# adaLN, Mamba2 and binarized FFN in one kernel: layer norms applied by ScalarE, gates' rows on other engines and another queue, weight tiles a step later

## The chip, the cores and the metric

The kernel runs on one core of a Trainium2 chip. A core has TensorE (PE; its weight load is shown apart as PEld), VectorE (DVE), ScalarE (ACT), GpSimd (POOL) and SyncE (SP). Each takes its instructions in order from its own queue; they meet through semaphores. Transfers are issued by SyncE, and a few by GpSimd and ScalarE, and are carried out by 16 DMA engines. The metric is device time in microseconds (us); lower is better. The time before is 733.64 us, the median of three runs between 733.6 and 734.45.

## The reference

There are 4 batches of 512 tokens with 512 features, all float32. With a modulation vector of six parts per batch (sa, ca, ga, sb, cb, gb), the block computes:

```
mod = (silu(c) @ wmod) -> sa, ca, ga, sb, cb, gb
ga = (2*(ga >= 0) - 1) * maximum(abs(ga), 0.25)      # gb likewise
h = layernorm(x) * (1 + ca) + sa
x = x + ga * mamba(h)
h = layernorm(x) * (1 + cb) + sb
x = x + gb * ffn(h)
layernorm(x) = (x - mean) / sqrt(var + 1e-5)
mamba(h): xBCzA = h @ in_proj.T;  xBC = silu(conv4(xBC) + bias)
          y = chunk scan with chunks of 128, decays exp(segsum(-softplus(A)))
          out = (y + D * x / dt) * silu(z + z_bias) @ out_proj.T
ffn(h):   bw = where(w >= 0, 1, -1) * mean(abs(w), per row);  h @ bw.T + bias
```

There are 64 heads of 16, 8 groups with a state of 64, an inner width of 1024, and a convolution over 2048 channels.

## The kernel before, in words

The 2048 tokens are worked in 8 halves (`h`) of 256 tokens; two halves make a batch. A half has two chunks of 128 (`c` = 0 and 1), and the scan of a chunk is cut into four units (`gp`), so there are 64 units, one per step of the main loop. Python lists (`FIRST`, `SECOND`, `FRONT`, and the calls of `at` behind them) say which other piece of work is laid into which step; the program is then put in order at build time, engine by engine, and runs in that order.

The front of half h+1 runs beside the scan of half h: load of x (`load_x`, L79), layer norm (`f_norm`, L307; it calls `layer_norm`, L289), four transposes on TensorE (`phT`, L330), modulation on ScalarE (`hT`, L347), dt (`f_dt`: `pa`, L368, then a chain of small VectorE work), projections B, C, x0 to x3 in pairs (`pp_B`, `pp_C`, `pp_x`, L434), each followed by ScalarE's first tap (`u_B`, `u_C`, `u_x`, L450), three VectorE taps per tile (L454), tanh (L458) and a product (L459). The z projections are evacuated by ScalarE (`uz`, L516; `thz`, L520). `xs` (L507) is a product on GpSimd with rows `rr` that SyncE loads (L502).

A unit (`stage0`, `stage1`, `stage2`) loads two decay tiles (SyncE, L541 and L542), takes 16 exponentials of 128x128 (ScalarE, L549, eight per tile), multiplies by the masked C-B products (VectorE, L625, once per tile), and multiplies with x on TensorE (`py`, L212 and L215). `yt` and `z` follow on VectorE and GpSimd (L666 to L675). Four decay tiles exist, so two units are in flight. The state rows `e` are loaded by SyncE (L582).

The tail of a chunk: `tail1` (L729) makes the out projection `po` (L739), `t = po * gates` (L742), the residual sum (L743), the layer norm of one tile, and adds the gated FFN bias on GpSimd (L745); `tail2` transposes (`ph`, L757) and modulates (`h`, L759); `tail3` makes `pf` (L775) and the output. The tails of chunk c=0 and of c=1 lie in the units that follow them.

`layer_norm` runs its statistics on VectorE (L295, L296), adds the epsilon (L297), takes the power -0.5 on GpSimd (`rs_a`, `rs_f`, L298), and applies both mean and scale on VectorE (L300). There are 32 applies of 128x512: 16 on x, two per half, and 16 on t, one per chunk.

Near the start, beside half 0, `late_mods` (L233) makes the other four modulation parts (`pg`, `rows`, `pm`) and then the gates' rows: five VectorE operations on 64x512 (L256 to L260) and three stores to `gate_d` in DRAM on the SyncE queue (L262). `load_gates` (L719) reads them back, broadcast, into `gates`. `load_wout` (L265) loads the out projection. `signs` (L269) loads a block of FFN weight rows `fw` (L272), sums their absolute values (`alpha`, L274), takes the sign (L277) and scales it on ScalarE (`sw`, L278); `turned_signs` (L281) transposes it into `bwT`.

What one bank of PSUM each holds (`mm` tiles: projections, transposes, po, pf) goes round five buffers, handed out in program order: a TensorE product waits until the readers of the tile five back are done. The steps around the change are set by these lines:

```
at(1, behind, 0, late_mods)
at(2, load_wout)
for o in range(NK):
    at(o // 2 + 2, signs, o)
...
for o in range(NK):
    at(o // 2 + 5, behind, 1, turned_signs, o)
```

Of the kernel before, what the change touches and what calls it, by code (L numbers as in the profile page):

```python
# [11 lines left out]
F32 = mybir.dt.float32  # L12
AF = mybir.ActivationFunctionType
# [3 lines left out]
P = 128  # L17
# [23 lines left out]
def adaln_mamba_block(  # L41
# [139 lines left out]
    def load_late(h):  # L181

        load_wm_at(2, wout[:, 0:NK])
        load_wm_at(5, wout[:, NK:])
        load_wm_at(4, bwT)
        for k in range(2):
            load_wm_at(3, room_z[k].unsqueeze(1), k)
        load_wm_at(3, room[:, 0:2, :], 2)


    sc = keep.tile([P, NK, 32], F32, name="sc")
# [41 lines left out]
    def late_mods(h):  # L233

        pg = ps.tile([P, DM], F32, tag="mm", name="pg")
        glued([
            partial(
                mm, pg[32 * j : 32 * j + 32, :], sc[:, k, :], wms[t6, k], start=(k == 0), stop=(k == NK - 1)
            )
            for k in range(NK) for j, t6 in enumerate((2, 5, 4, 3))  # L240
        ])
        row = wk.tile([P, DM], F32, tag="t", name="rows", bufs=1)
        nc.vector.tensor_copy(row, pg)
        pm = ps.tile([P, NK, P], F32, tag="mm", name="pm")
        for dt in range(NK):
            nc.tensor.transpose(pm[:, dt, :], row[:, dt * P : (dt + 1) * P], ident)
        nc.vector.tensor_copy(modT[:, 2], pm[:, :, 96 : 96 + B])
        nc.vector.tensor_scalar(modT[:, 3], pm[:, :, 64 : 64 + B], 1.0, None, ALU.add)

        g = row[0:64, :]  # L250
        sg = wk.tile([64, DM], F32, tag="h2", name="sg")
        ab = wk.tile([64, DM], F32, tag="h2", name="ab")
        brow = wk.tile([64, DM], F32, tag="th", name="brow")
        second = slice(32, 32 + B)
        nc.sync.dma_start(brow[second, :], ffn_b.partition_broadcast(B))
        nc.vector.tensor_scalar(sg, g, 0.0, 2.0, ALU.is_ge, ALU.mult)  # L256
        nc.vector.scalar_tensor_tensor(ab, g, -1.0, g, ALU.mult, ALU.max)
        nc.vector.tensor_scalar(ab, ab, 0.25, None, ALU.max)
        nc.vector.scalar_tensor_tensor(sg, sg, -1.0, ab, ALU.add, ALU.mult)
        nc.vector.tensor_mul(ab[second, :], sg[second, :], brow[second, :])  # L260
        for i, v in enumerate((sg[0:B, :], sg[second, :], ab[second, :])):
            nc.sync.dma_start(gate_d[:, i, :], v)  # L262

    def load_wout():
        nc.sync.dma_start(wout, w_outT.rearrange("(k p) e -> p k e", p=P))  # L265
# [23 lines left out]
    def layer_norm(tiles, name, into=None):  # L289
        n = len(tiles)  # L290
        st = wk.tile([P, n, 6], F32, tag=f"st{n}", name=f"st_{name}")
        mv = wk.tile([P, n, 2], F32, tag=f"mv{n}", name=f"mv_{name}")
        rs = wk.tile([P, n], F32, tag=f"rs{n}", name=f"rs_{name}")
        for j, t in enumerate(tiles):
            nc.vector.bn_stats(st[:, j, :], t)  # L295
            nc.vector.bn_aggr(mv[:, j, :], st[:, j, :])  # L296
        nc.vector.tensor_scalar(rs, mv[:, :, 1], EPS, None, ALU.add)  # L297
        nc.gpsimd.tensor_tensor(rs, rs, mhalf[:, :n], ALU.pow)  # L298
        for j, t in enumerate(tiles):
            nc.vector.tensor_scalar(  # L300
                into[j], t, mv[:, j, 0:1], rs[:, j : j + 1], ALU.subtract, ALU.mult
            )


# [512 lines left out]
    for h in range(NHALF):  # L817
# [4 lines left out]
        if h == 0:  # L822
            at(0, load_late, h)
            at(1, behind, 0, late_mods)
            at(2, load_wout)
            for o in range(NK):
                at(o // 2 + 2, signs, o)
    for o in range(NK):
        at(o // 2 + 5, behind, 1, turned_signs, o)
    for h in range(NHALF):  # L830
# [75 lines left out]
```

## Time and profile before

| what | value |
|---|---|
| median of three runs | 733.64 us |
| the profiled execution, its own time | 737.38 us |
| span of the profile | 735.7 us |
| mean granted TensorE clock | 0.993 |
| busy TensorE, VectorE, ScalarE, GpSimd | 700.4, 599.5, 522.0, 254.8 us |
| layer norm applies on VectorE (L300) | 11.5 us in 16 (t), 9.8 us in 16 (x) |
| VectorE idle before the t applies, waiting for GpSimd's power | 12.8 us in 16 |
| exponentials of the decays on ScalarE (L549) | 293.9 us in 960 |

The profile is one execution; every row has a start or a sum in microseconds. A busy share is an average over stages. An idle time is put down to what ended last before it ended, "waiter <- releaser". Matmuls are pipelined, so a busy TensorE is not one at its peak; the granted clock is given beside it by stage. The profiled execution is 0.5% longer than the median; 1.7 us of it lie outside the span.

### The profile page before, as it was taken

Reading aid. Unit: us, or ns where it says so; the run is one execution under the profiler, and the core shown is the slowest. Engines: PE = TensorE matmul, PEld = TensorE weight load, DVE = VectorE, ACT = ScalarE, POOL = GpSimd, SP = SyncE. Lnnn points to the kernel's source line nnn. Section 1 sums busy time; section 2 is a strip of 40 time slices with the busy share of each in tenths; the row PEclk is TensorE's granted clock in tenths of the full one; section 3 lists DMA queues with packets and bytes.
Section 4 is the critical chain, followed back from the end, with each engine's and each line's share of the span. In section 5 each row is a group of like instructions: output and inputs, shape, how many; then the busy total and the mean of one; then the engine's idle time right before and its main releaser. Section 6 shows DMA issues by size and latency. Waiting matters only on the chain.

```text
span 735.7 us, 15007 instructions
## 1 busy us (share of the span) xinstructions
PE 700.4 (95%) x5196; PEld 500.8 (68%) x5196; DVE 599.5 (81%) x1170; ACT 522.0 (71%) x1507; POOL 254.8 (35%) x297
## 2 busy tenths in 40 slices
PE   6999979899999999999999999999999999999997
PEld 3786746666677666677677666776667866677754
DVE  3869888876998678986899768996799867996995
ACT  2467658748696697785976787865968768788941
POOL 4021323444243332343223342433414332333652
PEclk9999989999999999999999999999999999999999
DMA  8991693535555256444644256552564537457720
GB/s 279 328 291 41 204 208 85 135 98 142 127 132 144 63 155 137 102 115 102 159 116 130 53 116 168 142 137 53 140 132 114 130 86 176 116 150 151 142 69 29
DMA packets 119067, 99.24 MB, mean 135 GB/s; under 512 B 73984, under 2 KB 97152, under 8 KB 118992
## 3 DMA queue, kind: packets, MB, share of 16 engines
q1 hardware_dynamic: 117808, 96.39, 52.3%
q0 software_dynamic: 896, 1.38, 0.7%
q8 instruction: 41, 0.67, 0.4%
q10 hardware_dynamic: 288, 0.52, 0.2%
q14 instruction: 34, 0.28, 0.1%
HBM read 92.47 MB, written 5.79 MB: 134 GB/s over the span
## 4 chain that ended last, share of the span: by engine, by line
PE 65%; ACT 16%; DVE 9%; DMA 4%; issue 4%; POOL 1%; SPq 1%; ACTq 0%; DVEq 0%; POOLq 0%
PE po L739 14%; PE pp_x L434 11%; PE pp_z L434 10%; ACT decay L549 9%; PE pp_C L434 7%; PE pp_B L434 5%; PE pf L775 3%; PE py L212 2%; PE py L215 2%; DVE decay L625 2%; ACT h L759 2%; DVE u_x L454 2%; DMA fw<-in_ffn_w 2%; ACT win L549 2%; PE gy L215 2%
## 5 line engine op out<-in xcount | busy, mean ns | idle before, releaser
L549 ACT ACTIVATE decay<-decay,st 128x128 f32<-128x128 f32 x960 | 293.9, 395 | 4.2 <-DMA decay<-sums_d 3.7
L625 DVE SCALAR_TENSOR_TENSOR decay<-decay,gm 128x1024 f32<-128x1024 f32 x120 | 160.8, 1341 | 50.3 <-ACT decay L549 47.2
L434 PE MATMUL pp_x<-hT,win 128*128 128x259 f32 x512 | 120.7, 390 | 7.3 <-DVE u_C L454 7.3
L434 PE MATMUL pp_z<-hT,win 128*128 128x256 f32 x512 | 118.1, 383 | 0.0
L434 PEld LDWEIGHTS pp_x<-hT,win 128*128 128x128 f32 x512 | 96.9, 193 | 25.2 <-ACT decay L549 7.7
L739 PE MATMUL po<-wout,z 128*128 128x512 f32 x256 | 113.8, 595 | 0.0
L434 PEld LDWEIGHTS pp_z<-hT,win 128*128 128x128 f32 x512 | 94.3, 189 | 16.3 <-issue 3.5
L675 POOL TENSOR_TENSOR z<-yt,z 128x256 f32<-128x256 f32 x62 | 62.9, 1015 | 76.1 <-DVE yt L674 57.8
L454 DVE SCALAR_TENSOR_TENSOR u_x<-pp_x,cw,u_x 128x256 f32<-128x256 f32 x192 | 83.6, 474 | 1.3 <-ACT u_x L450 0.7
L739 PEld LDWEIGHTS po<-wout,z 128*128 128x128 f32 x256 | 47.5, 190 | 53.1 <-issue 52.4
L672 POOL TENSOR_TENSOR yt<-yt,xs 128x256 f32<-128x256 f32 x46 | 41.4, 899 | 106.3 <-DVE yt L671 78.6
L507 POOL TENSOR_TENSOR xs<-u_x,rr 128x512 f32<-128x512 f32 x32 | 42.7, 1334 | 79.2 <-DVE u_x L459 61.3
L516 ACT ACTIVATE uz<-pp_z,zb 128x256 f32<-128x256 f32 x64 | 27.5, 470 | 59.0 <-PE pp_z L434 59.0
L215 PE MATMUL py<-decay,xpad 128*32 128x128 f32 x1680 | 66.3, 276 | 0.0
L434 PE MATMUL pp_B<-hT,win 128*128 128x259 f32 x256 | 63.5, 396 | 2.7 <-ACT decay L549 1.9
L434 PE MATMUL pp_C<-hT,win 128*128 128x259 f32 x256 | 59.6, 384 | 1.1 <-DVE u_x L454 1.1
L775 PE MATMUL pf<-bwT,h 128*128 128x512 f32 (+1 forms) x136 | 59.0, 578 | 1.4 <-ACT h L759 1.3
L434 PEld LDWEIGHTS pp_B<-hT,win 128*128 128x128 f32 x256 | 47.4, 193 | 14.5 <-ACT decay L549 3.1
L450 ACT ACTIVATE u_x<-pp_x,cb,cw 128x256 f32<-128x256 f32 x64 | 35.3, 560 | 30.5 <-PE pp_x L434 30.4
L434 PEld LDWEIGHTS pp_C<-hT,win 128*128 128x128 f32 x256 | 47.8, 189 | 9.4 <-PE pn L424 1.4
L679 POOL TENSOR_TENSOR xd<-xpad,st 128x256 f32<-128x256 f32 x48 | 34.1, 727 | 55.8 <-PE pst L215 28.3
L212 PE MATMUL py<-decay,xpad 128*32 128x128 f32 x240 | 47.4, 279 | 3.2 <-issue 2.2
(157 smaller groups left out, 1080.9 us busy)
## 6 DMA issues: line engine op xcount, KB each, us to landing
decay<-sums_d SPq DMA_DIRECT2D x120, 256.0 KB
decay<-sums_d SPq DMA_DIRECT2D x120, 128.0 KB
rr<-r_d SPq DMA_DIRECT2D x64, 128.0 KB
e<-e_d SPq DMA_DIRECT2D x96, 64.0 KB
win<-in_w_inT SPq DMA_DIRECT2D x4, 1024.0 KB
xr<-in_x SPq DMA_DIRECT2D x16, 256.0 KB
res<-o SPq DMA_DIRECT2D x15, 256.0 KB
x<-in_x SPq DMA_DIRECT2D x14, 256.0 KB
```

The source lines that it names most:

```text
L212: first = products[0]()
L215: product()
L434: last = mm(pm, win[:, k, col : col + P], H[h]["hT"][:, k, lo:], start=(k == 0), stop=(k == NK - 1))
L450: nc.scalar.activation(u[:, j, :], pm[:, KS - 1 :], AF.Identity, bias=cb[:, t : t + 1], scale=cw[:, t, KS - 1 : KS])
L454: nc.vector.scalar_tensor_tensor(u[:, j, :], pm[:, k : k + T], cw[:, t, k : k + 1], u[:, j, :], ALU.mult, ALU.add)
L507: nc.gpsimd.tensor_tensor(xs, xc, rr, ALU.mult)
L549: nc.scalar.activation(ets[r][:, i, :], ets[r][:, i, :], AF.Exp, bias=H[h]["st"][:, hd : hd + 1], scale=-1.0)
L625: nc.vector.scalar_tensor_tensor(ets[r], ets[r], 1.0, bc_mid(gm[:, r, :], HPG), ALU.min, ALU.mult)
L672: ew.tensor_add(t, t, xs)
L675: ew.tensor_mul(zg, t, zg)
L739: last_po = mm(po, H[h]["z"][g // 2][:, g % 2, c * CH : (c + 1) * CH], wout[:, g, :], start=(g == 0), stop=(g == NKI - 1))
L775: mm(pf, h2[:, k, :], bwT[:, k, cols], start=(k == 0), stop=(k == NK - 1))
```

## The change

Three things change. First, every layer norm but the very first (`a0`) is applied by ScalarE as `rs * t + nm` with a per-partition bias `nm = -mean * rs`. VectorE makes `-mean`, GpSimd multiplies it by `rs` after the power, and ScalarE applies. Second, the gates' rows leave `late_mods` for a function of their own, `late_gates`, one step later: VectorE does the sign, ScalarE the absolute value, GpSimd the three others, and the stores go through GpSimd's queue; the work stands in the `gates` buffer (`room`) itself, and the load of the FFN bias row moves to `load_late`. Third, `signs` runs one step later; `turned_signs` stays.

In the program order built from it, ScalarE's t apply in a c=0 tail of halves 1 to 6 stands after the first exponential of the next unit's first decay tile. The x applies and the t of c=1 stand between `thz_1` and `uz_2`. In half 1's front the order on ScalarE is: the absolute value, eight exponentials, the two x applies, eight exponentials, `uz_3`, `xpad`, `thz_3`, eight exponentials, the first `hT`, eight exponentials, the other three `hT`. On TensorE, `pf` of a c=0 tail stands ahead of `gy` in five halves, and the PSUM buffers are handed out anew.

```diff
--- before.py
+++ after.py
@@ -186,6 +186,7 @@
         for k in range(2):
             load_wm_at(3, room_z[k].unsqueeze(1), k)
         load_wm_at(3, room[:, 0:2, :], 2)
+        nc.sync.dma_start(brow[second, :], ffn_b.partition_broadcast(B))
 
 
     sc = keep.tile([P, NK, 32], F32, name="sc")
@@ -246,20 +247,28 @@
             nc.tensor.transpose(pm[:, dt, :], row[:, dt * P : (dt + 1) * P], ident)
         nc.vector.tensor_copy(modT[:, 2], pm[:, :, 96 : 96 + B])
         nc.vector.tensor_scalar(modT[:, 3], pm[:, :, 64 : 64 + B], 1.0, None, ALU.add)
-
-        g = row[0:64, :]
-        sg = wk.tile([64, DM], F32, tag="h2", name="sg")
-        ab = wk.tile([64, DM], F32, tag="h2", name="ab")
-        brow = wk.tile([64, DM], F32, tag="th", name="brow")
-        second = slice(32, 32 + B)
-        nc.sync.dma_start(brow[second, :], ffn_b.partition_broadcast(B))
-        nc.vector.tensor_scalar(sg, g, 0.0, 2.0, ALU.is_ge, ALU.mult)
-        nc.vector.scalar_tensor_tensor(ab, g, -1.0, g, ALU.mult, ALU.max)
-        nc.vector.tensor_scalar(ab, ab, 0.25, None, ALU.max)
-        nc.vector.scalar_tensor_tensor(sg, sg, -1.0, ab, ALU.add, ALU.mult)
-        nc.vector.tensor_mul(ab[second, :], sg[second, :], brow[second, :])
+        late_row.append(row)
+    late_row = []
+    second = slice(32, 32 + B)
+    brow = room[0:64, 2, :]
+    def late_gates(h):
+        g = late_row.pop()[0:64, :]
+        sg, ab = room[0:64, 0, :], room[0:64, 1, :]
+        nc.vector.tensor_scalar(sg, g, 0.0, 0.5, ALU.is_ge, ALU.subtract)
+        nc.scalar.activation(ab, g, AF.Abs)
+        nc.gpsimd.tensor_scalar(ab, ab, 0.25, 2.0, ALU.max, ALU.mult)
+        nc.gpsimd.tensor_tensor(sg, sg, ab, ALU.mult)
+        nc.gpsimd.tensor_tensor(ab[second, :], sg[second, :], brow[second, :], ALU.mult)
         for i, v in enumerate((sg[0:B, :], sg[second, :], ab[second, :])):
-            nc.sync.dma_start(gate_d[:, i, :], v)
+            nc.gpsimd.dma_start(gate_d[:, i, :], v)
 
     def load_wout():
         nc.sync.dma_start(wout, w_outT.rearrange("(k p) e -> p k e", p=P))
@@ -295,10 +304,21 @@
             nc.vector.bn_stats(st[:, j, :], t)
             nc.vector.bn_aggr(mv[:, j, :], st[:, j, :])
         nc.vector.tensor_scalar(rs, mv[:, :, 1], EPS, None, ALU.add)
+        if name == "a0":
+            nc.gpsimd.tensor_tensor(rs, rs, mhalf[:, :n], ALU.pow)
+            for j, t in enumerate(tiles):
+                nc.vector.tensor_scalar(
+                    into[j], t, mv[:, j, 0:1], rs[:, j : j + 1], ALU.subtract, ALU.mult
+                )
+            return
+        nm = wk.tile([P, n], F32, tag=f"nm{n}", name=f"nm_{name}")
+        nc.vector.tensor_scalar(nm, mv[:, :, 0], -1.0, None, ALU.mult)
         nc.gpsimd.tensor_tensor(rs, rs, mhalf[:, :n], ALU.pow)
+        nc.gpsimd.tensor_mul(nm, nm, rs)
         for j, t in enumerate(tiles):
-            nc.vector.tensor_scalar(
-                into[j], t, mv[:, j, 0:1], rs[:, j : j + 1], ALU.subtract, ALU.mult
+            nc.scalar.activation(
+                into[j], t, AF.Identity, bias=nm[:, j : j + 1], scale=rs[:, j : j + 1]
             )
 
 
@@ -823,8 +843,9 @@
             at(0, load_late, h)
             at(1, behind, 0, late_mods)
             at(2, load_wout)
+            at(2, late_gates, h)
             for o in range(NK):
-                at(o // 2 + 2, signs, o)
+                at(o // 2 + 3, signs, o)
     for o in range(NK):
         at(o // 2 + 5, behind, 1, turned_signs, o)
     for h in range(NHALF):
```

## The prediction

> **What bounds the kernel now.** First the page's busy rows (engine, microseconds, share of the span, instructions): TensorE is busy nearly all the time, so only its gaps can be won, and anything that makes a new gap is lost.
>
> ```profile
> PE 700.4 (95%) x5196; PEld 500.8 (68%) x5196; DVE 599.5 (81%) x1170; ACT 522.0 (71%) x1507; POOL 254.8 (35%) x297
> ```
>
> Second, what TensorE waits for (waiter <- last releaser: total us, times, longest). These four lines are rows 1, 3, 5 and 10 of that view:
>
> ```profile
> PE pp_x L434 <- DVE u_C L454: 7.3, 2, 5.4
> ...
> PE pa L368 <- ACT hT L347: 3.3, 8, 0.6
> ...
> PE pp_B L434 <- ACT decay L549: 1.9, 3, 0.6
> ...
> PE pp_C L434 <- DVE u_x L454: 1.1, 2, 0.6
> ```
>
> The 7.3 us are two stalls near the start (5.4 and 1.9). The rest are small and come back in every half. The chain that ended last, between 82 and 106 us, shows where the 5.4 comes from (start, us, what): SyncE issues the first FFN weight rows, their transfer takes 13.38 us, VectorE waits for it at `alpha` (L274), and the C convolution behind that wait keeps a PSUM buffer from the next x projection.
>
> ```profile
> 82.26 0.76 SPq L272
> ...
> 83.06 13.38 DMA fw<-in_ffn_w
> ...
> 98.08 1.19 DVE u_C L454 x3
> 99.27 0.14 issue
> 99.41 6.23 PE pp_x L434 x16
> ```
>
> The sixteen records of pp_x take 6.23 us there and 3.70 elsewhere, and the table by stage (window, length, busy time of PE, PEld, DVE, ACT, POOL, then the granted clock) says why: after the gap the clock is 0.50. The stall costs 5.4 + 2.5 = 7.9 us.
>
> ```profile
> 94.00:99.00 5.00, 0.05 (x2) 0.00 (x0) 3.56 (x8) 2.57 (x6) 1.18 (x2) 0.86 1.06 250
> 99.00:103.00 4.00, 3.60 (x9) 2.87 (x10) 4.00 (x9) 2.10 (x7) 0.00 (x0) 0.50 1.06 265
> ```
>
> Third, the timeline of ScalarE and VectorE in the tail of a first chunk (c=0) in the steady part, 372 to 390 us (start, us, row, idle before). It is where the moved `t` apply lands:
>
> ```profile
> 377.95 2.44 ACT L549 ACTIVATE decay<-decay,st 128x128 f32<-128x128 f32 x8
> 380.29 0.55 ACT L450 ACTIVATE u_x<-pp_x,cb,cw 128x256 f32<-128x256 f32 x1
> 380.99 0.56 ACT L450 ACTIVATE u_x<-pp_x,cb,cw 128x256 f32<-128x256 f32 x1 [0.15 <-PE pp_x L434]
> 381.45 2.44 ACT L549 ACTIVATE decay<-decay,st 128x128 f32<-128x128 f32 x8
> ...
> 384.44 1.49 ACT L759 ACTIVATE h<-ph,modT 128x128 f32<-128x128 f32 x4
> ```
> ```profile
> 379.37 0.95 DVE L300 TENSOR_SCALAR t<-xr,mv_f,rs_f 128x512 f32<-128x512 f32 x1 [1.04 <-POOL rs_f L298]
> ```
>
> ScalarE has no gap there, VectorE has one (1.04), waiting for GpSimd's power.
>
> **Norms on ScalarE.** Thirty applies leave VectorE (14 x at 654 ns, 16 t at 719 ns: 20.7 us) and with them the waits in front of them (t 12.8 us in 16). Added: 23 `nm` on VectorE (rs_f's row, 143 ns: 3.3 us), 23 products on GpSimd, 30 applies on ScalarE. The product has no row. Below stands the copy of 128x12 (0.19 us), above the power of 128x1 (0.56); I take 0.35. The apply's nearest row is `sw` (L278, Identity with a per-partition scale, 128x512): 723 ns, so 21.7 us on ScalarE. Its bounds are th_x, 627 ns, and twice the 723.
>
> The Trainium skill ("ScalarE: Activation LUTs", section "What ACT_TABLE_LOAD costs") charges about 93 ns for each per-partition pointer operand, and this apply has two, bias and scale. By that rule my estimate of one apply is 186 + 2 x 93 + 0.833 x 512 = 0.80 us, 2.3 us more over the thirty and 0.5 us more in the six tails below; the rows 627 (none) and 723 (one) agree with the step.
>
> *Where ScalarE idles* the applies cost nothing. The 14 x applies and the t of second chunks stand, in the new order, after thz_1 and before uz_2, where ScalarE waits 53.1 us in 12 times for pp_z between 140 and 700 us. If that cover were gone, three applies would cost 2.2 us per half.
>
> *In the c=0 tails of halves 1 to 6* they are not covered. The new order on ScalarE is: u_x of tile 1, one exponential of the first decay tile, **t**, the other seven, th_x, eight exponentials of the second tile, and only then the u_x of tiles 2 and 3, and h. t waits at the head of the queue for GpSimd: power done at 379.34, product at 379.7, so ScalarE stands still from 378.3 to 379.7 and gives 0.72 to t. Then 2.14 + 0.55 + 2.45 brings the second tile to 385.6, the u_x to 386.6 (381.5 before), h to 388.1 (385.9). VectorE multiplies the second decay tile first (1.21, from 385.6), then runs the convolutions of x tiles 2 and 3 (six by 0.41). Two things that TensorE needs are late: pn waits for h (its PSUM buffer), and pp_C for the third convolution of x tile 2, about 386.8 + 5 x 0.41 = 388.8. Before, pp_C started at 387.26. So +1.5 us in an odd half. In an even half the power comes after z (t at 292.04): the same working gives pp_C at 301.65 against 300.49, +1.15. Three of each: **+8.0**. Ends: 0 (the scheduler's slack elsewhere swallows it), and 2.4 a half (stand-still 1.7 and apply 0.72 both fully on TensorE's path), 14.4.
>
> *VectorE's relief.* TensorE's waits for VectorE between 140 and 700 us are pp_C's 1.1 and py's 0.7. That is all the relief can give there: **-1.5**, ends 0 and -1.8.
>
> *The last tail.* The chain st_f, rs, power, apply, ph, h, pf is bare. Product 0.35 and apply 0.72 against 0.55: **+0.5**, ends 0.3 and 1.0.
>
> **Start (64 to 110 us).** Gates' rows and weight tiles belong here. VectorE loses sg, ab, ab, sg, ab (0.42, 0.68, 0.41, 0.67, 0.99) and gets one of 0.42: 2.75 us off. The rest goes to ScalarE (one Abs of 64x512, about 0.55) and GpSimd (three, nearest rows 0.62 for a 64x512 memset and 1.34 for a 128x512 product; about 3 us), and three DMA issues of 0.55 move from SyncE to GpSimd, in front of xs of tile 2. SyncE is no longer held by `ab` (the two waits on L262, 4.8 and 3.7 us), w_out is issued about 69 instead of 81.79, and the weight rows come one step later, behind e, the gates' load and the next decay loads. So `alpha` no longer stands in front of the C convolution with its data missing: **-5.4**. The gates' load waits for GpSimd's DMAs until about 82; its first reader is near 108. The bias row's load (0.29) goes to an early step, and the tiles' own rows (alpha 0.68, sw 0.42 and 0.72) stay the same and come later; their first reader, turned_signs, two or three steps on, covers them (uncovered: 1.8 a tile).
>
> But half 1's norm moves too. ScalarE's order becomes Abs, 8 exponentials, x, x, 8 exponentials, uz_3, xpad, thz, 8 exponentials, first hT, 8 exponentials, three hT. Before, hT came directly after thz and was done at 79.2. Power took 2.55 us here (71.79), 0.71 in all the other rows of that shape; then comes one of the gates' operations, then the product: x starts between 72.8 and 74.4, hT ends between 85.5 and 87.1. pa and the first B projection wait for hT; the B projection ends at 88.2 to 89.8 instead of 83.29: +4.9 to +6.5, I take **+5.7**. The later C convolutions then hold pp_x for 0 to 1.8: **+0.9**. The clock: TensorE idles 4 to 6 us before hT. Gaps of 1.9 (130 us) leave the clock at 1.00, the one of 5.4 brought 0.50. This one is nearer to the second, so the 2.5 us move and are not won: **0**, ends -2.5 and 0.
>
> The Trainium skill ("TensorE: Matmul & The Clock Gate", part 1, on the clock gate) puts the drop at an idle window of about 3.4 us, which speaks against this change: by it the new gap also halves the clock, and the sum stays.
>
> In half 0's tail GpSimd has xs (1.28) between power and product, which delays ph by 1.3 to 2.4, while the stall of 1.9 near 130 us should go: **0**, ends -2.3 and +2.4. Start together +1.2, ends -5.1 and +5.
>
> **Sum.** 8.0 - 1.5 + 0.5 + 1.2 = 8.2 on the profiled execution's 737.38. I take off 0.7 for gaps later in a half that shrink when TensorE comes late (pa's wait for hT, 2.7 us in 6, could give half of that at most): +7.5. The profiled run is 3.7 above the median of 733.64; its gaps are the same sort, so +7.5 on the median: 741.1.
>
> **Rivals.**
> A, *faster*: one mechanism, ScalarE's waits for GpSimd lie beside TensorE's work. ScalarE runs its queue in order, but five PSUM buffers stand between it and TensorE; where they are not all full, late u_x, h and hT delay nothing. For it: ScalarE is busy 71% only, VectorE 81%, and TensorE is idle for 35 us in all, of which the new waits could fill old ones. Against: pn and pp_C reuse the buffers of exactly the late rows. Its price is the 8.0 of the tails and the 5.7 + 0.9 of hT, and without the gap before hT the 2.5 us of half clock are won as well: 7.5 - 14.6 - 2.5 = -9.6, 724.0. It decides from the point where the waits cost less than half of the 14.6 us: 7.5 - 7.3 is no change, and the clock makes it a gain.
> B, *slower than the forecast*: in the c=0 tails ScalarE is TensorE's only source of free buffers, so stand-still and apply come through in full, 14.4 for 8.0: 7.5 + 6.4 = +13.9, 747.5. For it: ScalarE shows no gap from 377.95 to 385.9; against: six convolutions in front of pp_C give some room. It decides if pp_C starts over 2 us later in each tail.
> C, *no change*: half of the waits are covered, the start's gain and the tails' loss meet: 733.8.
>
> **How the numbers follow.** 0.2% (1.5 us) is about what a measurement of this kernel can tell from no change. Forecast 0.48 (its own range 736 to 745), A 0.27 (722 to 732), C 0.08, B 0.17 (745 to 751). The range cuts A and B at their outer parts, about 0.1 each: 726 to 749. Faster 0.28, same 0.08, slower 0.64.
>
> **What would show it.** VectorE near 580 us, ScalarE near 544, GpSimd near 265. TensorE's list loses pp_x <- u_C 5.4 and gets pa <- hT or phT with 4 us or more near 80; in the c=0 tails pn <- h and pp_C <- u_x with over 1 us, six times; ScalarE waits for nm_f by about 1.5. Wrong if hT of half 1 ends before 82, if the clock stays at 1.00 around 85, or if pp_C in the tails starts less than half a microsecond later.

## The result: slower by 2.9%, and the profile after

The changed kernel takes 754.52 us (median of 4 runs, 752.68 to 759.09); beside it the kernel before took 734.05 (733.6 to 735.5). The ratio is 1.0285, with a 95% interval of 1.0237 to 1.0333. The forecast was 741.1 with a range up to 749: the direction was right, the size was not.

The busy row of the changed kernel's page has VectorE and ScalarE where the prediction put them (580 and 544), and GpSimd at 275 for 265:

```profile
PE 703.0 (93%) x5196; PEld 500.5 (66%) x5196; DVE 580.1 (77%) x1159; ACT 543.5 (72%) x1538; POOL 275.1 (37%) x326
```

So the work moved as foreseen; TensorE's share fell from 95 to 93%, and the loss is in its gaps. To see where, I cut the span at the same work in each kernel: the first z projection (35.1 us before, 33.5 after), the first `hT` of half 2 (181.4, 181.1), the first `hT` of half 7 (613.0, 625.3) and the end. The profiled execution of before began 1.6 us late and that is left out of the stretches: its granted clock is 0.50 from 15.73 to 19.14 us. Three other executions below have the same dip and a first projection at 35.0 to 35.3 us; the other twelve have neither.

| stretch | holds | before | after | difference |
|---|---|---|---|---|
| start | half 0, gates' rows, first weight tiles | 146.3 | 147.7 | +1.4 |
| middle | the c=0 tails of halves 1 to 5 | 431.6 | 444.2 | +12.6 |
| last | the c=0 tail of half 6, half 7, the end | 122.7 | 127.5 | +4.8 |

The sum, before rounding, is +18.7; the profiled executions differ by 17.1 (754.46 against 737.38), which is 18.7 less the late 1.6. In the middle an interval that holds the tail of an odd half grew from 85.0 to 87.7 us, one with the tail of an even half from 88.3 to 90.5. In the last stretch 2.2 came before the last full `pf`, about what an even half's tail costs, and 2.5 after it. The six c=0 tails thus cost 12.6 + 2.2 = 14.8 us. That is most of it.

TensorE's waits in the changed kernel (waiter <- last releaser: total us, times, longest), rows 1 and 3 to 7 of that view:

```profile
PE pa L388 <- ACT hT L367: 8.9, 8, 5.9
...
PE pn L439 <- ACT h L779: 5.3, 6, 1.6
PE pp_C L454 <- DVE u_x L474: 5.1, 6, 1.2
PE ph L777 <- ACT t L320: 4.4, 2, 3.4
PE pf L795 <- DVE u_B L474: 4.1, 5, 1.1
PE pp_B L454 <- DVE S L732: 2.4, 3, 0.8
```

`pp_x <- u_C` with its 5.4 is gone and `pa <- hT` with 5.9 has come, as predicted for the start. The third, fourth, sixth and seventh rows of the view are the tails'. Against before they add 5.3 + (5.1 - 1.1) + 4.1 + 2.4 = 15.8 us. Three small waits of the same tails are no longer there: `pp_B <- decay` 1.9, `pp_B <- h` 0.7, `pn <- h` 0.4. So 12.8 of the 14.8 are accounted for by these rows.

One odd tail, that of half 1, on ScalarE, in the timeline of the changed kernel (start, us, row, idle before it):

```profile
203.94 0.56 ACT L470 ACTIVATE u_x<-pp_x,cb,cw 128x256 f32<-128x256 f32 x1 [0.67 <-PE pp_x L454]
204.40 0.39 ACT L569 ACTIVATE decay<-decay,st 128x128 f32<-128x128 f32 x1
206.10 0.81 ACT L320 ACTIVATE t<-xr,nm_f,rs_f 128x512 f32<-128x512 f32 x1 [1.31 <-POOL nm_f L318]
206.82 2.14 ACT L569 ACTIVATE decay<-decay,st 128x128 f32<-128x128 f32 x7
208.86 0.61 ACT L478 ACTIVATE th_x<-u_x 128x512 f32<-128x512 f32 x1
209.38 2.43 ACT L569 ACTIVATE decay<-decay,st 128x128 f32<-128x128 f32 x8
211.72 1.00 ACT L470 ACTIVATE u_x<-pp_x,cb,cw 128x256 f32<-128x256 f32 x2
212.62 1.48 ACT L779 ACTIVATE h<-ph,modT 128x128 f32<-128x128 f32 x4
```

The same place in the timeline of before (u_x of tile 1 starts at 204.18 there), where `u_x` of x tiles 2 and 3 stands between the two decay tiles:

```profile
206.99 0.55 ACT L450 ACTIVATE u_x<-pp_x,cb,cw 128x256 f32<-128x256 f32 x1
207.69 0.56 ACT L450 ACTIVATE u_x<-pp_x,cb,cw 128x256 f32<-128x256 f32 x1 [0.15 <-PE pp_x L434]
208.16 2.44 ACT L549 ACTIVATE decay<-decay,st 128x128 f32<-128x128 f32 x8
```

The stand-still is 1.31 and the apply 0.81, but the `u_x` of tiles 2 and 3 come at 211.72 instead of 206.99: they stand behind eight more exponentials. TensorE in the changed kernel, same tail:

```profile
214.16 0.33 PE L439 MATMUL pn<-ident,sh 128*128 128x128 f32 x1 [1.60 <-ACT h L779]
...
215.35 3.74 PE L454 MATMUL pp_C<-hT,win 128*128 128x259 f32 x16 [0.49 <-DVE u_x L474]
218.94 0.60 PE L487 MATMUL pt_xt<-ident,u_x 128*128 128x128 f32 x4
220.59 3.70 PE L795 MATMUL pf<-bwT,h 128*128 128x512 f32 x8 [1.06 <-DVE u_B L474]
```

and before:

```profile
213.97 3.74 PE L434 MATMUL pp_C<-hT,win 128*128 128x259 f32 x16 [0.57 <-DVE u_x L454]
...
218.63 0.61 PE L215 MATMUL gy<-C,B 64*128 64x128 f32 x8
219.17 3.70 PE L775 MATMUL pf<-bwT,h 128*128 128x512 f32 x8
```

`pn` waits 1.60 for `h`. Counted from the first `hT` of half 2 (181.13 and 181.37), pp_C starts 1.63 us later than before, near the +1.5 worked out; in even halves it is 1.76 for +1.15. The second piece was not worked out: `pf` stands ahead of `gy` now, and waits 1.06 for the B convolution that holds its PSUM buffer. In even halves there are two more: the B projection waits 0.79 for `S`, and `pf` 0.46. The tail of half 2 in the changed kernel:

```profile
300.62 2.02 PE L454 MATMUL pp_B<-hT,win 128*128 128x259 f32 x8 [0.79 <-DVE S L732]
...
309.38 2.84 PE L795 MATMUL pf<-bwT,h 128*128 128x512 f32 x6 [0.46 <-DVE u_B L474]
```

At the start the table by stage (window, length, busy time of PE, PEld, DVE, ACT, POOL, granted clock, DMA share, GB/s) shows the new gap before `hT` and a clock that falls with it:

```profile
76.00:84.00 8.00, 3.28 (x14) 1.87 (x16) 4.17 (x4) 8.00 (x25) 6.41 (x7) 0.64 0.31 114
84.00:88.00 4.00, 4.00 (x22) 2.70 (x20) 1.59 (x5) 1.44 (x4) 0.00 (x0) 0.87 0.00 0
```

At the end, the last tail in the timeline:

```profile
742.26 0.66 PE L777 MATMUL ph<-ident,t 128*128 128x128 f32 x4 [1.02 <-ACT t L320]
...
743.52 5.41 PE L795 MATMUL pf<-bwT,h 128*128 128x256 f32 x16 [0.61 <-ACT h L779]
```

Statistics to `pf` takes 4.16 us here (739.36 to 743.52) and 3.63 before: the predicted half microsecond. The other 1.7 of the end is the last `pf` itself, 5.41 for 3.72.

### The profile page after: what moved, and what is told of

Same layout as the page of the kernel before. It is cut to its first block, busy times and chain, and to the rows that moved or that the text cites. A ratio compares the mean times of both kernels' runs of the same rounds, so it can differ in the third digit from the quotient of the medians.

```text
span 752.8 us, 15038 instructions
## 1 busy us (share of the span) xinstructions
PE 703.0 (93%) x5196; PEld 500.5 (66%) x5196; DVE 580.1 (77%) x1159; ACT 543.5 (72%) x1538; POOL 275.1 (37%) x326
## 4 chain that ended last, share of the span: by engine, by line
PE 57%; ACT 19%; DVE 17%; issue 5%; POOL 1%; DMA 1%; ACTq 0%; DVEq 0%; SPq 0%; POOLq 0%
PE po L759 12%; ACT decay L569 11%; PE pp_z L454 11%; PE pp_x L454 9%; DVE decay L645 4%; PE pp_B L454 4%; PE pf L795 4%; PE pp_C L454 3%; PE py L213 2%; PE py L216 2%; DVE u_x L474 2%; ACT h L779 2%; PE gy L216 1%; PE pa L388 1%; PE pt_xt L487 1%
## 5 line engine op out<-in xcount | busy, mean ns | idle before, releaser
L645 DVE SCALAR_TENSOR_TENSOR decay<-decay,gm 128x1024 f32<-128x1024 f32 x120 | 163.7, 1365 | 72.6 <-ACT decay L569 70.5
L454 PE MATMUL pp_x<-hT,win 128*128 128x259 f32 x512 | 118.2, 385 | 0.0
L759 PE MATMUL po<-wout,z 128*128 128x512 f32 x256 | 115.4, 602 | 0.0
L454 PEld LDWEIGHTS pp_x<-hT,win 128*128 128x128 f32 x512 | 95.1, 189 | 16.9 <-issue 1.8
L695 POOL TENSOR_TENSOR z<-yt,z 128x256 f32<-128x256 f32 x62 | 63.8, 1028 | 87.1 <-DVE yt L694 54.4
L692 POOL TENSOR_TENSOR yt<-yt,xs 128x256 f32<-128x256 f32 x46 | 46.9, 1020 | 105.5 <-DVE yt L691 65.7
L795 PE MATMUL pf<-bwT,h 128*128 128x512 f32 (+1 forms) x136 | 60.7, 593 | 5.2 <-DVE u_B L474 4.1
L699 POOL TENSOR_TENSOR xd<-xpad,st 128x256 f32<-128x256 f32 x48 | 37.5, 797 | 57.0 <-ACT xpad L513 39.0
L454 PEld LDWEIGHTS pp_C<-hT,win 128*128 128x128 f32 x256 | 47.8, 189 | 13.3 <-DVE u_x L474 4.0
L320 ACT ACTIVATE t<-xr,nm_f,rs_f 128x512 f32<-128x512 f32 x16 | 13.0, 813 | 59.7 <-POOL nm_f L318 59.7
```

Source lines behind the costliest of these rows:

```text
L454: last = mm(pm, win[:, k, col : col + P], H[h]["hT"][:, k, lo:], start=(k == 0), stop=(k == NK - 1))
L645: nc.vector.scalar_tensor_tensor(ets[r], ets[r], 1.0, bc_mid(gm[:, r, :], HPG), ALU.min, ALU.mult)
L692: ew.tensor_add(t, t, xs)
L695: ew.tensor_mul(zg, t, zg)
L699: nc.gpsimd.tensor_tensor(xd, xg, by_head(H[h]["ed"][:, hd0 : hd0 + HPP]), ALU.mult)
L759: last_po = mm(po, H[h]["z"][g // 2][:, g % 2, c * CH : (c + 1) * CH], wout[:, g, :], start=(g == 0), stop=(g == NKI - 1))
```

## The experiments

The theory after the result: the tails lose because ScalarE, which works its queue in order, holds `u_x` and `h` back, and the queue's new *order* matters more than the 0.81 us of an apply. Rivals: the stand-still for GpSimd itself, the apply's own time, or something outside the tails. For the start: the gains and losses of the three parts add up as in the prediction, or they don't. All stretches below are cut as above. The kernel before was run again beside each of four groups of these runs, with medians of 736.07, 735.65, 735.72 and 736.18; each ratio is against the runs beside it. A stretch's length comes from one profiled execution, and the start of one and the same program differed by 3 us with the granted clock (the last section shows this), so small differences of starts say little.

### The t applies back on VectorE

An edit in the changed kernel's layer norm:

```diff
-        if name == "a0":
+        if name == "a0" or name[0] == "f":
```

> The changed kernel with the 16 t applies back on VectorE (no nm for them); x applies on ScalarE, gates and weight tiles as changed. Tail theory (ScalarE's stand-still at t in the c=0 tails is what costs): TensorE loses pn <- h, pp_C <- u_x, pf <- u_B in the tails, 14 us come back, and 2 to 3 at the end; the late hT of half 1 stays: 735 to 738 us. Rival (the x applies, or the new order of everything, cost as well): 742 us or more.

Measured: 737.65, ratio 1.002 (1.0008 to 1.0032); start 147.8, middle 431.4, last 122.9. The sixteen t applies, with the order that came with them, are all of the loss behind the start. The fourteen x applies on ScalarE cost nothing there, and win nothing.

### Only the c=0 applies back on VectorE

The same place, for the tails of c=0 alone:

```diff
-        if name == "a0":
+        if name == "a0" or (name[0] == "f" and name[-1] == "0" and name != "f0_0"):
```

> The changed kernel with only the t applies of first chunks (halves 1 to 7) back on VectorE; x applies and the t of second chunks stay on ScalarE. Tail theory: all of the 14 us come back, half a microsecond at the end stays: 737 to 741 us. Rival (the t of second chunks and x cost the same each): 745 us or more.

Measured: 739.49, ratio 1.0054 (1.0033 to 1.0075); start 147.4, middle 431.3, last 124.7. The middle is that of before to 0.3 us: the loss there belongs to the c=0 tails, and the relief of VectorE by the x applies and the t of c=1 is worth 0.3 us, not 1.5.

### The norms alone

The layer norm of the changed kernel in the kernel before, with its gates and weight tiles.

```diff
...
-            nc.vector.tensor_scalar(
-                into[j], t, mv[:, j, 0:1], rs[:, j : j + 1], ALU.subtract, ALU.mult
+            nc.scalar.activation(
+                into[j], t, AF.Identity, bias=nm[:, j : j + 1], scale=rs[:, j : j + 1]
             )
...
```

> The kernel before with only the norms changed; gates' rows, their stores and the weight tiles as before. Tail theory: the same 14 us in the tails and 3 at the end, and at the start hT late by 3 to 6 us with the stall of 5.4 on the weight rows still there: 751 to 760 us. Rival (the gates' rows on ScalarE and GpSimd carry the loss): under 745 us.

Measured: 758.57, ratio 1.0305 (1.0276 to 1.0333); start 150.3 (+4.0), middle 444.9 (+13.3, with two dips of the clock that before does not have), last 125.5. The same tails, and a worse start than with the two other parts.

### The order alone

The kernel before, where the first taps of x tiles 2 and 3 wait in ScalarE's queue until the second decay tile's exponentials are issued, as in the changed kernel. No instruction is added and t stays on VectorE.

```diff
+            late = newest.get(("exp", h - 1, 1, 2)) if name == "x1" and h > 1 else None
+            with tc.issue_after(late.ins) if late else nullcontext():
-            nc.scalar.activation(
+                nc.scalar.activation(
...
```

> The kernel before, all norms on VectorE, nothing added; only the first-tap evacuations of x tiles 2 and 3 are queued behind the second decay tile's exponentials in the c=0 tails, as the changed kernel has them, from half 1 on. If the order is the cause: 6 to 10 us over the kernel before, with pp_C <- u_x or pn <- h in TensorE's list. If it only costs together with the stand-still: under 3 us.

Measured: 750.88, ratio 1.019 (1.0162 to 1.0218); middle 445.3, +13.7. TensorE's first wait in that kernel:

```profile
PE pp_C L434 <- DVE u_x L456: 12.0, 6, 2.3
```

Part of this is the clock: it is 0.50 from 216.91 to 220.32 and from 394.40 to 397.81, and the two intervals that hold these dips took 89.3 and 89.1 us where the third of their kind took 87.9. Without the dips the middle would be about 11 us longer than before, an estimate. So two rows moved back in a queue cost nearly as much as the whole change costs in the middle, and more than the 6 to 10 us expected. It is not the same loss in detail: VectorE still has the t apply here, and most of the wait falls on pp_C.

### The order undone in the changed kernel

The first taps of the x tiles are handed out ahead of the exponentials again:

```diff
+            with tc.high_priority(offset=200) if name in ("x0", "x1") and h > 1 else nullcontext():
-            nc.scalar.activation(
+                nc.scalar.activation(
...
```

> The changed kernel, with the first-tap evacuations of x tiles 0 to 3 raised in priority for halves 2 to 7, so that they stand among the first tile's exponentials, ahead of the second tile's, while t keeps its place and its wait. If the order is the cause: 8 to 12 of the 14 us in the tails come back, 742 to 746 us. If stand-still and apply are: 1 to 4 us come back, 750 to 753.

Measured: 743.48, ratio 1.0108 (1.0078 to 1.0137); start 150.6, middle 434.6, last 124.9. Its ScalarE in the tail of half 1 still stands still and still applies, but the `u_x` come early:

```profile
209.86 0.81 ACT L320 ACTIVATE t<-xr,nm_f,rs_f 128x512 f32<-128x512 f32 x1 [1.26 <-POOL nm_f L318]
210.58 0.39 ACT L570 ACTIVATE decay<-decay,st 128x128 f32<-128x128 f32 x1
210.87 0.55 ACT L471 ACTIVATE u_x<-pp_x,cb,cw 128x256 f32<-128x256 f32 x1
211.32 1.26 ACT L570 ACTIVATE decay<-decay,st 128x128 f32<-128x128 f32 x4
212.49 0.55 ACT L471 ACTIVATE u_x<-pp_x,cb,cw 128x256 f32<-128x256 f32 x1
```

Of the 12.6 us in the middle 3.0 are left. With stand-still and apply in place, the order was worth 9.6, three quarters. The rows `pf <- u_B` and `pp_B <- S` are no longer in TensorE's list between 182 and 700 us.

### The wait alone

The kernel before, with a reading of `rs` by ScalarE in the same six tails. Nothing uses its result; t stays on VectorE.

```diff
         nc.gpsimd.tensor_tensor(rs, rs, mhalf[:, :n], ALU.pow)
+        if name[0] == "f" and name[-1] == "0" and name[1] not in "07":
+            probe = wk.tile([P, n], F32, tag="probe", name=f"probe_{name}")
+            nc.scalar.activation(probe, rs, AF.Identity)
```

> The kernel before, with t on VectorE, and in the c=0 tails of halves 1 to 6 one extra ScalarE instruction (Identity of 128x1 into a scratch tile) that waits for the power; it stands after the first exponential of the first decay tile, and both u_x still stand ahead of the second tile's exponentials. If the stand-still for GpSimd is the cause (1.0 to 1.3 us each): 6 to 9 us over the kernel before. If the order of u_x behind the second tile's exponentials is the cause: under 2.5 us over it.

Measured: 741.84, ratio 1.0077 (1.0051 to 1.0102); middle 435.5, +3.9. In the tail of half 1:

```profile
203.68 0.20 ACT L301 ACTIVATE probe_f<-rs_f 128x1 f32<-128x1 f32 x1 [0.85 <-POOL rs_f L298]
203.79 2.14 ACT L552 ACTIVATE decay<-decay,st 128x128 f32<-128x128 f32 x7
205.84 1.00 ACT L453 ACTIVATE u_x<-pp_x,cb,cw 128x256 f32<-128x256 f32 x2
206.74 2.44 ACT L552 ACTIVATE decay<-decay,st 128x128 f32<-128x128 f32 x8
```

By the medians this is 6.2 us over the kernel before, at the lower edge of the first expectation; in the stretches with the six tails it is 5.4. So the stand-still costs something by itself: the wait, 0.85 in this tail, costs a third of the middle's loss in a queue where `u_x` keeps its place ahead of the second decay tile.

### The apply's time alone

The kernel before, with a 128x512 activation of two pointer operands in the same tails, on data that is there without a wait for GpSimd. Nothing uses its result.

```diff
+        if name[0] == "f" and name[-1] == "0" and name[1] not in "07":
+            probe = wk.tile([P, DM], mybir.dt.bfloat16, tag="probe", name=f"probe_{name}", bufs=1)
+            nc.scalar.activation(probe, tiles[0], AF.Identity, bias=mv[:, 0, 0:1], scale=mv[:, 0, 1:2])
```

> The kernel before, with t on VectorE, and in the same six tails one extra ScalarE Identity of 128x512 from the residual into a scratch tile, which waits for the statistics only and not for GpSimd; the u_x of x tile 2 stands ahead of the second tile's exponentials, that of x tile 3 behind them. If 0.7 us of ScalarE time is what comes through: about 4 us over the kernel before. If only stand-still or the full reordering cost: under 2 us.

Measured: 740.39, ratio 1.006 (1.0039 to 1.008); middle 436.3, +4.7, which is 0.9 us for each of the five tails there. The time is not quite alone: in this order the `u_x` of x tile 3 stands behind the second tile's exponentials, as the expectation says, so how much the 0.80 us of the instruction cost by themselves is not shown. Wait and apply make 8.6 together, but only 3.0 with VectorE relieved and `u_x` early: the costs don't add.

### The weight tiles alone, a step later and two steps later

```diff
-                at(o // 2 + 2, signs, o)
+                at(o // 2 + 3, signs, o)
```

> The kernel before with only the weight tiles one step later; norms and gates' rows as before. VectorE's order puts all C convolutions of half 1 ahead of alpha, and hT stays early on ScalarE. If alpha and its wait held the C convolution: pp_x <- u_C falls from 5.4 to under 2 and the half clock goes, 726 to 730 us. If VectorE's other work (dt chain, decay products) holds it: 731 to 734 us.

Measured: 731.77, ratio 0.9939 (0.9922 to 0.9956): **faster than both kernels**. The start is 139.9, 6.4 us shorter; the middle is unchanged (432.0). TensorE's wait for `u_C` in that kernel:

```profile
PE pp_x L434 <- DVE u_C L454: 1.9, 1, 1.9
```

and its table by stage, for the stretch that ran at clock 0.50 before:

```profile
99.00:103.00 4.00, 4.00 (x10) 1.85 (x11) 3.69 (x8) 2.84 (x9) 1.31 (x2) 1.00 1.07 174
```

The gap of 5.4 before that pp_x became 1.9, and the half clock went with it: 3.5 + 2.5 us against the profiled execution of before, whose 737.38 is above the medians of that kernel (734.05 to 736.18); by the medians the gain is 3.9. The signs are those of the first expectation, the time is in the range of the second. The prediction counted the whole 5.4, because a transfer of 13.38 stood in the chain. But VectorE had been idle for the transfer for 1.49 + 0.32 us only, and `alpha` and `sw` themselves took 2.2.

Two steps later:

```diff
-                at(o // 2 + 2, signs, o)
+                at(o // 2 + 4, signs, o)
```

> As tiles_later, with the weight tiles two steps later than before. If alpha and its wait held the C convolution, the same gain as tiles_later within 1.5 us, since both stand behind the C convolutions; if turned_signs then waits for the tiles, 2 to 4 us over tiles_later.

Measured: 735.14, ratio 0.9999 (0.9981 to 1.0016); start 144.2. Now TensorE waits for `sw` (1.3), for `pbw` behind `h` (1.5) and, in pp_x, for a decay tile (2.3). Of the two, one step is better, by 3.4 us.

### The gates alone

The gates' rows of the changed kernel; norms and weight tiles as before.

```diff
...
+            at(2, late_gates, h)
             for o in range(NK):
                 at(o // 2 + 2, signs, o)
```

> The kernel before with only the gates' rows changed (ScalarE, GpSimd and GpSimd's queue); weight tiles and norms as before. If the gates' rows are what made gates_and_tiles slow (new order of hT, dt chain and alpha): 738 to 745 us. If it was the later tiles: 732 to 736 us.

Measured: 740.60, ratio 1.0064 (1.0042 to 1.0086); start 151.6, +5.3. ScalarE at the first `hT`:

```profile
75.33 0.56 ACT L356 ACTIVATE hT<-phT,modT 128x256 f32<-128x256 f32 x1
75.78 2.44 ACT L558 ACTIVATE decay<-decay,st 128x128 f32<-128x128 f32 x8
78.12 1.01 ACT L356 ACTIVATE hT<-phT,modT 128x256 f32<-128x256 f32 x2
79.02 2.45 ACT L558 ACTIVATE decay<-decay,st 128x128 f32<-128x128 f32 x8
81.36 0.56 ACT L356 ACTIVATE hT<-phT,modT 128x256 f32<-128x256 f32 x1
```

Sixteen exponentials of 0.3 us stand among the four `hT`, which end at 81.9 for 79.2 before. That order looks worse for TensorE, but it does not explain the +5.3. In this execution the clock is 0.50 for 17.1 us of the start, for 6.8 in before; the kernel of "The gates with their stores on SyncE's queue" below has the same `hT` among the same exponentials, only 3.4 us at 0.50, and a start of 146.9.

### Gates and weight tiles

The changed kernel with the layer norm of before:

```diff
...
-            nc.scalar.activation(
-                into[j], t, AF.Identity, bias=nm[:, j : j + 1], scale=rs[:, j : j + 1]
+            nc.vector.tensor_scalar(
+                into[j], t, mv[:, j, 0:1], rs[:, j : j + 1], ALU.subtract, ALU.mult
             )
```

> The kernel before with the gates' rows and the weight tiles changed, all norms applied on VectorE as before. Tail theory: no tail cost; the stall of 5.4 us on the weight rows and its half clock of 2.5 go: 726 to 729 us. Rival (the start gives nothing, because hT is late by the gates' rows on GpSimd in any case): 733 to 737 us.

Measured: 744.19, ratio 1.0108 (1.008 to 1.0135). A clear miss: start 154.3, +8.0, middle and last as before. `alpha` has no wait for its data any more, but VectorE is busy without a gap from 90 to 110 us, and the dt chain, which starts when `hT` and `pa` are done, begins at 86.01 instead of 80.58 and stands among the convolutions. Here too the clock is 0.50 from 77.73 to 84.56, where before has it at 1.00, and 17.1 us of the start are at 0.50. TensorE's two long waits in that kernel:

```profile
PE pp_x L443 <- DVE u_C L463: 5.5, 1, 5.5
PE pp_x L443 <- ACT xpad L502: 4.4, 1, 4.4
```

and its VectorE in the timeline where the first ends:

```profile
99.67 0.47 DVE L463 SCALAR_TENSOR_TENSOR u_C<-pp_C,cw,u_C 128x256 f32<-128x256 f32 x1
100.06 1.21 DVE L634 SCALAR_TENSOR_TENSOR decay<-decay,gm 128x1024 f32<-128x1024 f32 x1
101.20 0.67 DVE L283 TENSOR_REDUCE alpha<-fw 128x1 f32<-128x512 f32 x1
...
103.05 0.47 DVE L463 SCALAR_TENSOR_TENSOR u_C<-pp_C,cw,u_C 128x256 f32<-128x256 f32 x1
```

The last tap of `u_C` again stands behind a decay product, two `alpha` and two `sw`, now with their data present. The 5.5 us stall needs no DMA.

### The same, with `hT` and the dt chain of half 1 first

```diff
+                with tc.high_priority(offset=300) if h == 1 else nullcontext():
+                    nc.scalar.activation(
+                        hT[:, dt, KS - 1 :], pt[:, q, :], AF.Identity,
...
-(2, f_dt, ())
+(2, first_dt, ())
```

> The kernel before with gates' rows and weight tiles changed (as in gates_and_tiles, 744.2), all norms on VectorE, and half 1's hT and dt work raised in priority, so that hT stands behind 14 exponentials and the absolute value of pa behind 16 and no longer behind 32. If the order of hT and dt is why the gates' rows cost at the start: 12 to 15 us come back, 729 to 732 us, level with or under tiles_later (731.8). If the gates' work on GpSimd and ScalarE itself costs: 736 to 741 us.

Measured: 736.12, ratio 1.000 (0.9986 to 1.0013); start 145.8. So 8.5 us of start come back with the new order, and the clock that stays at 1.00 around 80 us is a part of them (6.8 us of the start are at 0.50, for 17.1). The 139.9 of the weight tiles by themselves is not reached, and the time is in the range of the second expectation. What keeps the other 5.9 is open; its waits are new ones (pp_x for `u_B` 4.0, for `xpad` 2.3).

### The gates with their stores on SyncE's queue

The kernel of "the gates alone", with one line as it was before:

```diff
-            nc.gpsimd.dma_start(gate_d[:, i, :], v)
+            nc.sync.dma_start(gate_d[:, i, :], v)
```

> As gates_alone (740.6), but with the three stores of the gates' rows back on SyncE's queue. ScalarE's order of hT and exponentials is the same as in gates_alone. If that order is the cause: 739 to 742 us again. If the change of queue (freed SyncE, stores in front of xs on GpSimd) is the cause: 735 to 737 us.

Measured: 739.33 (736.86 to 742.69), ratio 1.0043 (1.0025 to 1.0062); start of the profiled execution 146.9. The runs spread over both expectations, and the spread goes with the mean granted clock: 736.86 to 737.55 at 0.995 to 0.997, 741.77 to 742.69 at 0.988. "The gates alone" has 738.51 at 0.995, and 742.47 and 742.83 at 0.988, so at the same clock the queue is worth about 1 us or less. From 78 to 86 us, first that kernel, then this one (the last numbers are the clock, the DMA share and GB/s):

```profile
78.00:86.00 8.00, 7.27 (x26) 4.71 (x26) 2.63 (x2) 3.92 (x12) 5.96 (x6) 0.58 0.01 3
78.00:86.00 8.00, 7.50 (x71) 5.30 (x72) 4.78 (x7) 5.19 (x15) 3.42 (x3) 1.00 0.17 60
```

### The changed kernel with c=0 on VectorE and an early `hT`

```diff
+        if name in ("a0", "f7_1") or (name[0] == "f" and name[-1] == "0"):
...
+            with tc.high_priority(offset=300) if name == "a1" else nullcontext():
...
+                with tc.high_priority(offset=300) if h == 1 else nullcontext():
```

> The changed kernel with the t applies of c=0 and of the last chunk on VectorE, and half 1's x applies and hT raised in priority on ScalarE, so that hT stands four exponentials after the x applies and no longer behind 24. If the late hT is what eats the start's gain: pa <- hT falls from 5.9 to under 3, and the start is 3 to 6 us shorter: 729 to 733 us. If VectorE is what holds the start: pp_x <- u_C comes back in its place, and 734 to 738 us.

Measured: 743.71, ratio 1.0106 (1.0081 to 1.0131): slower than with the c=0 applies alone moved back, and a miss of both expectations. `pa` waits only 2.1 for `hT`, but pp_x now waits 4.4 for `xpad` and 2.9 for `u_C`, and `pn` 1.9 for `sw`; the start is 152.2, with 13.7 us of it at a clock of 0.50. Where the gap before `hT` shrank, other waits took its place.

## Why the prediction was wrong, step by step

| step | predicted | measured |
|---|---|---|
| c=0 tails of halves 1 to 6 | +8.0 (0 to 14.4) | +14.8, with the relief in it |
| VectorE's relief | -1.5 | -0.3 (c=0 applies back on VectorE) |
| gaps that absorb | -0.7 | 0 (pa's waits for `hT` between 182 and 700 us: 2.7 in 6, before and after) |
| last tail | +0.5 | +0.5, and 2.0 more at the end, 1.7 of it clock |
| start | +1.2 | +1.4 |

**The step that failed is "Three of each: +8.0".** Its mechanism is right, and shown: with the order undone 9.6 of 12.6 us come back, and the order alone costs 13.7, some 11 of it without the clock's dips. Its two places were right as well. `pn <- h` and `pp_C <- u_x` add 4.9 + 4.0 us, 6.3 after the 2.6 of small waits on pp_B that they replace; I had 8.0. What was mis-sized is the rest of the tail, priced at nothing: `pf <- u_B` 4.1 and `pp_B <- S` 2.4, together 6.5 us. By position, pp_C starts 1.63 us later in each odd tail and 1.76 in each even one, 10.2 in six, and 4.6 come behind it. That `pf` stands ahead of `gy` in five halves had been read from the program order and was written down as a fact of the change, but no price was put on it. Before, `gy` filled 218.08 to 219.17 in front of `pf`; that it would have covered the wait of 1.06 is argued from this, not run.

**Relief and absorption** are hardly there. The first assumes that TensorE's small waits shrink when VectorE is freer: the kernel with c=0 back on VectorE has all the relief outside these tails, and its middle is 0.3 us shorter. The second assumes that pa's waits shrink when TensorE comes late: they did not.

**The start's sum was right and its terms were not.** By stretches, the weight tiles alone give -6.4 (I had -5.4, without the clock), the gates alone +5.3 (I had none apart from `hT`'s place), both +8.0, the norms alone +4.0, all three +1.4. These don't add, so +1.2 against +1.4 is no proof of the working: that they agree is luck. The clock is in all of them, as the table in the last section shows; by the medians against the runs beside them the weight tiles alone give -3.9, the gates alone +4.9 and both +8.1. My 0 for the clock was near: 10.2 us of the changed kernel's start are at 0.50 for 6.8 before, which costs 1.7 us at most. What held: the 5.4 stall went; `hT`, expected to end between 85.5 and 87.1, ended at 84.3; `pa` waited 5.9 us for it; and the clock fell there.

**The step to the median.** The profiled execution of before was 3.3 us above the median of the runs beside the changed kernel's, and I put that down to its gaps. Half of it, 1.6, was a late first projection behind a dip of the clock. The change's profiled execution lies on its median, so by medians the difference is 20.5 where the profiles have 17.1.

**The rivals.** A (waits beside TensorE's work) is refuted by the tails' +14.8, and by the wait alone and the apply alone, +3.9 and +4.7 in the five tails of the middle. B had the right price, 14.4 for the tails, but its condition did not come true: pp_C starts 1.63 to 1.76 us later, not over 2. The room in front of pp_C was there as I said; the loss that was missed came at `S` before it and at `pf` behind it. C is out.

**The apply's price.** ScalarE's apply measured 0.81 us where I took 0.72 from `sw`. The Trainium skill, "ScalarE: Activation LUTs", section "What ACT_TABLE_LOAD costs", gave an estimate of 0.80, which the trace confirms; over six tails it is half a microsecond. GpSimd's product took 0.19, for 0.35.

## What to carry to other kernels

Moving an instruction to another engine is priced by what stands behind it in that engine's queue, over the whole stretch until the last reader is served: go through every TensorE row of the new order there, not only the first that is late. A wait at the head of an in-order queue, and above all a new order of that queue, can cost more than the instruction (about 11 us with no instruction added, 9.6 won back with all of them in place). And a transfer in the chain is worth the idle time that it causes, 1.8 us here, not its 13.4; when parts of a change meet in one crowded stage, run them apart, since the best version was one line of this change (731.77). Then compare medians, or look at the clock of each stretch first: two profiled executions of the same instructions differed by 3 us in the start.

## What the runs showed of the hardware beyond that

The granted clock doesn't follow the length of a gap alone; it follows how busy TensorE was in fixed windows of 3.41 us. In the changed kernel a gap of 3.41 us before `ph` at 124.02 left it at 1.00; the window after the gap:

```profile
124.00:126.00 2.00, 1.98 (x42) 1.61 (x44) 1.54 (x5) 2.00 (x6) 1.29 (x1) 1.00 0.38 130
```

With only the weight tiles later, a gap of 1.93 before `ph` at 115.90 brought it down, as two rows of the table by stage show:

```profile
115.90:118.00 2.10, 2.10 (x14) 1.51 (x15) 2.10 (x6) 2.10 (x8) 2.07 (x3) 0.72 0.99 213
118.00:120.00 2.00, 2.00 (x6) 1.54 (x5) 2.00 (x5) 2.00 (x7) 1.38 (x1) 0.50 0.33 81
```

The sixteen pp_C behind it took 5.22 us there and 3.77 in the changed kernel. Likewise the last `pf` took 5.41 in the changed kernel and 3.72 with the norms alone, behind the same gaps of 1.02 and 0.61. The Trainium skill ("TensorE: Matmul & The Clock Gate", part 1) names an idle window of about 3.4 us and says that the window runs freely. The length fits the drops at 5.4 and 5.9, not these, and the measurement decides. That the window runs freely does fit: in each of the sixteen traces the stretches at 0.50, apart from one that the kernel's end cuts short, are 3.41, 6.83 or 10.24 us long, and all their edges lie on one grid with a step of 3.41 us.

But a window of that grid need not be idle. From 25 us on, the traces have 3104 grid windows at full clock. In 28 of them TensorE's records cover less than 0.41 of the window, and the window behind was at 0.50 every time. In 29 they cover 0.41 to 0.53, and 12 were followed by 0.50; of the 3047 above, none was. So what counts is where the grid cuts a gap. The 3.41 before `ph` in the changed kernel are cut at 122.60, with TensorE busy for 1.43 and 1.99 us of the two windows, and the clock stayed; the 1.93 with the weight tiles later fell into one window that was busy for 1.48 of 3.41. At the last `pf` the window is busy for 1.78 in the changed kernel and for 1.84 with the norms alone, close to the border on either side. My value of nothing for the clock behind a gap of 1.9 was too sure.

This is also why starts spread. The table has the time at 0.50 inside the start of the profiled executions that are compared above; half of it is the most that it can have cost, and less where TensorE waits anyway.

| kernel | start | of it at 0.50 |
|---|---|---|
| before | 146.3 | 6.8 |
| changed | 147.7 | 10.2 |
| c=0 applies back on VectorE | 147.4 | 10.2 |
| order undone in the changed kernel | 150.6 | 17.1 |
| norms alone | 150.3 | 10.2 |
| weight tiles one step, two steps later | 139.9, 144.2 | 3.4, 3.4 |
| gates alone | 151.6 | 17.1 |
| gates, stores on SyncE's queue | 146.9 | 3.4 |
| gates and weight tiles | 154.3 | 17.1 |
| the same, `hT` and dt chain first | 145.8 | 6.8 |
| changed, c=0 on VectorE and early `hT` | 152.2 | 13.7 |

Up to the end of the start, the kernels of the second, third and fourth row run the same instructions in the same order on TensorE, VectorE, ScalarE and GpSimd; the fourth row's start is 3 us longer, with 6.8 us more at 0.50.

GpSimd's power of 128x2 takes 0.70 to 0.71 us, but the second one of a run, near 70 us, took 2.55 to 2.61 in each kernel with the gates' rows as before. In those with the new gates' rows it took 0.70, and the gates' operation right behind it 1.94. Some 1.8 us stick to that place and not to the power; why is open.
